# A graph-attention layer and a graph convolution in one kernel: values by seven block products after the keys, and two running sums in the softmax

## The chip, the cores and the metric

The kernel runs on one core of a Trainium2 chip. A core has a matrix engine (TensorE, PE in the profile; PEld are its weight loads), a vector engine (VectorE, DVE), a scalar engine (ScalarE, ACT), GpSimd (POOL) and SyncE (SP), which here issues most DMAs. The metric is device time in microseconds, taken as the median of several runs. All arithmetic is fp32.

## The reference, cut to what matters

Input x has 16 batches of 1024 nodes with 256 channels; adj is 1024 x 1024. Two layers follow each other. The part that the change touches is in layer 0:

```python
h = relu(layernorm(x))
fea = h.transpose(0, 2, 1)                     # batch, channel, node
c_adj = mean(fea, axis=1)
diff = c_adj[:, None, :] - c_adj[:, :, None]
A = abs(abs(sigmoid(diff) - 0.5) - 0.5) * 2    # A_s = (A + A^T) / 2
g = relu(einsum('bcn,bnm->bcm', fea, adj * A_s) * para)
q = g by heads                                  # 4 heads of 64 channels
k, v = halves of h @ kv_w by heads              # kv_w is 256 x 512
out = softmax(q @ k^T * scale) @ v
x = x + out
```

Layer 1 normalises x again, multiplies it with the normalised adjacency matrix, then with W1 (512 x 256), applies a batch norm over all batches and nodes, a relu, W2 and another batch norm, and adds the result to x.

## The kernel before, in words

A first stage runs over the 16 batches and does layer 0 of each batch together with the adjacency product and W1 of the batch before; a second stage does the rest of layer 1, for which all batches must be done. The order of the instructions on every engine is written out by hand (a manual schedule): an engine executes its instructions in the order in which the code issues them, and buffers and semaphore waits are placed by the framework. A buffer of a pool is taken when its tile is first written, and is free again when the last reader of the tile before is done.

One turn of the batch loop has these steps.

- **Attention** (`attention`). There are four steps: two halves of the 512 queries times two pairs of heads. In each, `scores` makes eight blocks of 128 keys by 2 heads by 512 queries in PSUM (L743, two heads at once on half of PE's rows each), ACT takes the exponential into a tile p (L751), and DVE adds the eight tiles into one running sum (L757 for the first two, L760 for the six after). `partial` turns that sum in blocks of 32 (L768) and reduces it (L776). `values` in `attention` multiplies p with v (L784), and DVE turns the result (L797). The weights of the next batch's graph product are begun between (`hooks`: ACT at L353 and L356, DVE at L361).
- **The graph product of the next batch** (`graph_seven`, from the third batch on; `graph` for the first two). The product of h and the weights is made from six blocks in pairs, by seven products instead of eight (Strassen's method in Winograd's form: sums of the blocks are made on DVE, and one PSUM bank, f_gpsx, collects several products and is copied by ACT in between, at L641, L653 and L659). Its results are joined by DVE (L661, L664, L667) and multiplied with para into the queries (L670, L683).
- **Values and keys of the next batch**, at the end of `graph_seven`. Values come first: the function `values` at L443 takes 128-node blocks of h (turned, in hT) as the stationary operand and the 256 value columns of kv_w as the moving one, 16 matmuls of 256 columns in two PSUM tiles, which ACT copies (L458). Keys follow in seven products of 128 x 128 by 128 x 512 blocks (L691): sums of the key weights (`sums`, loaded by L537 from `kvs_d`, where `make_key_sums` puts them once, L1019) times sums of h (kt1 to kt4, made by DVE at L677 to L681). The bank f_kpsx collects four of these products and is copied by ACT after each (L707, L713, L718, L725); the next product into it waits for the copy. On ACT, the relu of the second layer norm (`norm.relu`, L281) stands before these copies; it needs `norm.shifts` (L266) of DVE.
- **Adjacency product and W1 of this batch** (`linear1`, L944, and `linear1_seven`, L1050), again by seven products. The layer norm of the batch after the next is prepared in it.

SP issues, in this order within `graph_seven`: loads of the sums, hT, para, the key sums and three adjacency sums; sixteen small DMAs that turn the attention result (f_att, L852); then, after the keys' second product, the store of the batch's x (`leave`, L1195) and a load of a later x (`arrive`, L191).

PSUM has one pool of three two-bank tiles (`ps_s`, used by scores, f_gps, f_vps, f_kpsx, the adjacency product) and two single banks (`ps_t` and `ps_o`). In SBUF the change touches the pools' tags "acc" (two buffers), "att" and "sums" (one each).

Of the kernel before, what the change touches and what calls it, by code (L numbers as in the profile page):

```python
# [10 lines left out]
F32 = mybir.dt.float32  # L11
# [6 lines left out]
P = 128  # L18
# [11 lines left out]
def fast_path(  # L30
# [20 lines left out]
    nc = tc.nc  # L51
# [3 lines left out]
    NC = N // P  # L55
# [7 lines left out]
    dram = ctx.enter_context(tc.tile_pool(name="fdram", bufs=1, space=DRAM))  # L63
# [3 lines left out]
    hT_d = [dram.tile([CC, P, N], F32, tag=f"fhT_{b}", name=f"fhT_{b}") for b in range(B)]  # L67
    gs_d = [dram.tile([P, 12, P], F32, tag=f"fgs_{b}", name=f"fgs_{b}") for b in range(B)]
    w1s_d = dram.tile([P, 4, FC * P // 2], F32, tag="fw1s", name="fw1s")
    kvs_d = dram.tile([P, 4, P], F32, tag="fkvs", name="fkvs")  # L70
    t_d = [dram.tile([P, 4, 512], F32, tag=f"ft_{k}", name=f"ft_{k}") for k in range(3)]
    z1_d = [dram.tile([P, FC, 512], F32, tag=f"fz1_{t}", name=f"fz1_{t}") for t in range(TT)]

# [102 lines left out]
    with ExitStack() as stage:  # L176
# [266 lines left out]
        def values(b, hT, v):  # L443

            copies = []
            for c4 in range(0, NC, 4):
                ps = ps_s.tile([P, 4, C], F32, tag="s", name=f"f_vps_{b}_{c4}")
                for i in range(4):
                    for e in range(CC):
                        nc.tensor.matmul(  # L450
                            ps[:, i, :],
                            hT[e][:, ts(c4 + i, P)],
                            kvw_t[:, e, C : 2 * C],
                            start=(e == 0),
                            stop=(e == CC - 1),
                        )
                copies.append(
                    lambda c4=c4, ps=ps: nc.scalar.copy(v[:, c4 : c4 + 4, :], ps)  # L458
                )
            return copies  # L460
# [40 lines left out]
        def graph_seven(b, left, norm, load_more, last):  # L501
# [32 lines left out]
                hT.append(t)  # L534
            qT = big.tile([P, CC, N], F32, tag="qT", name=f"f_qT_{b}")
            nc.sync.dma_start(qT, para_v)
            nc.sync.dma_start(sums, kvs_d)  # L537
            load_more()
            kT = big.tile([P, CC, N], F32, tag="kT", name=f"f_kT_{b}")
            v = big.tile([P, NC, C], F32, tag="v", name=f"f_v_{b}")  # L540
# [114 lines left out]
            m4(2)  # L655
            for n in range(PAIRS):
                m5(n)
            t23 = pp.tile([P, 2, 512], F32, tag="acc", name=f"f_kt23_{b}", bufs=2)
            nc.scalar.copy(room[:, 1], x)  # L659
            add0()  # L660
            nc.vector.tensor_add(room[:, 2], room[:, 2], m7)  # L661
            norm.stats(0, 4)
            norm.invert(0, 4)
            nc.vector.tensor_add(room[:, 3], room[:, 1], m7)  # L664
            both = lambda d: room[:, 2 * d : 2 * d + 2].rearrange("p n k -> p (n k)")
            for d in range(CC):
                nc.vector.tensor_add(both(d), both(d), gps[d])  # L667
# [1 line left out]
                ws.pop((b, c))  # L669
            nc.vector.tensor_mul(qT[:, 0, :], both(0), qT[:, 0, :])  # L670
            norm.shifts(0, 4)
            norm.relu(0, 4, False)
            copy0, copy1 = values(b, hT, v)
            copy0()
            kt2, kt3, kt4 = t23[:, 0], t23[:, 1], rest[:, 0]
            part = lambda k, j: hT[k][:, ts(j, 512)]
            nc.vector.tensor_sub(kt3, part(1, 1), part(0, 1))  # L677
            nc.vector.tensor_add(kt2, kt3, part(0, 0))
            nc.vector.tensor_sub(kt4, part(1, 0), kt2)
            kt1 = part(0, 1)  # L680
            nc.vector.tensor_sub(kt1, kt1, part(0, 0))  # L681
            add1()
            nc.vector.tensor_mul(qT[:, 1, :], both(1), qT[:, 1, :])  # L683
            norm.stats(4, NC)
            norm.invert(4, NC)


            aw = lambda i, k: kvw_t[:, k, ts(i, P)]

            def mult(ps, left, right, more=False):  # L690
                nc.tensor.matmul(  # L691
                    ps, left, right, start=not more, stop=True, skip_group_check=more
                )

            c = lambda i, j: kT[:, i, ts(j, 512)]
            x = ps_s.tile([P, 512], F32, tag="s", name=f"f_kpsx_{b}")
            m7 = ps_s.tile([P, 512], F32, tag="s", name=f"f_kps7_{b}")
            k2 = ps_t.tile([P, 512], F32, tag="t", name=f"f_kps2_{b}")
            k4 = ps_o.tile([P, 512], F32, tag="o", name=f"f_kps4_{b}")

            def relu_queries(d):

                nc.scalar.activation(qT[:, d, :], qT[:, d, :], AF.Relu, scale=-SCALE)

            todo = [lambda d=d: relu_queries(d) for d in range(CC)]
            mult(x, aw(0, 0), part(0, 0))
            nc.scalar.copy(c(0, 0), x)  # L707
            mult(k2, aw(0, 1), part(1, 0))
            nc.vector.tensor_add(c(0, 0), c(0, 0), k2)
            leave(b - 1)  # L710
            arrive(b + 1)
            mult(x, sums[:, 1], kt2, True)
            nc.scalar.copy(c(1, 0), x)  # L713
            todo.pop(0)()
            mult(m7, sums[:, 2], kt3)
            nc.vector.tensor_add(c(1, 0), c(1, 0), m7)
            mult(x, sums[:, 0], kt1, True)
            nc.scalar.copy(c(1, 1), x)  # L718
            copy1()
            mult(k4, aw(1, 1), kt4)  # L720
            nc.vector.tensor_add(c(1, 1), c(1, 1), m7)
            norm.shifts(4, NC)
            nc.vector.tensor_add(c(1, 0), c(1, 0), k4)
            mult(x, sums[:, 3], part(1, 1), True)
            nc.scalar.copy(c(0, 1), x)  # L725
            if last:
                todo.pop(0)()
            else:
                norm.relu(4, NC, False)
            return (qT, kT, v), todo  # L730

        def attention(b, qT, kT, v, hooks):

            steps = [(g, pair) for g in range(NH) for pair in range(HEADS // 2)]
            p_of, acc_of, oT_of, o_of, red_of = {}, {}, {}, {}, {}

            def scores(s, within=None):
                g, pair = steps[s]
                for m in range(NC):
                    ps = ps_s.tile([P, 2, 512], F32, tag="s", name=f"f_s_{b}_{s}_{m}")  # L740
                    for e in range(2):
                        rows_e = slice(e * HD, (e + 1) * HD)
                        nc.tensor.matmul(  # L743
                            ps[:, e, :],
                            kT[rows_e, pair, ts(m, P)],
                            qT[rows_e, pair, ts(g, 512)],
                            start=True,
                            stop=True,
                        )
                    p = pp.tile([P, 2, 512], F32, tag="p", name=f"f_p_{b}_{s}_{m}")  # L750
                    nc.scalar.activation(p, ps, AF.Exp)  # L751
                    p_of[s, m] = p
                    if m == 1:
                        acc = pp.tile(
                            [P, 2, 512], F32, tag="acc", name=f"f_acc_{b}_{s}", bufs=2
                        )
                        nc.vector.tensor_add(acc, p_of[s, 0], p)  # L757
                        acc_of[s] = acc
                    elif m > 1:
                        nc.vector.tensor_add(acc_of[s], acc_of[s], p)  # L760
                    if m == 5 and within:
                        within()

            def partial(s):

                g, pair = steps[s]
                t = ow.tile([P, 2, 16, 32], F32, tag="sums", name=f"f_sums_{b}_{s}")
                nc.vector.transpose(  # L768
                    t.rearrange("p e j i -> p (e j i)"),
                    acc_of.pop(s).rearrange("p e q -> p (e q)"),  # L770
                )
                if pair == 0:
                    red_of[g] = small.tile(
                        [P, HEADS // 2, 2, 16], F32, tag="red", name=f"f_red_{b}_{g}", bufs=1
                    )
                nc.vector.tensor_reduce(red_of[g][:, pair], t, AX.X, ALU.add)  # L776
# [89 lines left out]
            first = finish(0)  # L866
            collect, invert, spread, scale, add = first
            for i in range(len(steps)):
                scores(i, collect if i == 2 else None)
                for step in hooks.get(i, ()):  # L870
                    step()
                if i == 2:
                    invert()
                    spread()
                partial(i)
                if i == 2:
                    scale()
                values(i)
# [139 lines left out]

        def make_key_sums():  # L1019

            t = pp.tile([P, 2, 512], F32, tag="acc", name="f_kvs", bufs=2)
            s1, s2, s3, s4 = (t[:, 0, ts(n, P)] for n in range(4))
            a = lambda i, k: kvw_t[:, k, ts(i, P)]
            nc.vector.tensor_add(s1, a(1, 0), a(1, 1))
            nc.vector.tensor_sub(s2, s1, a(0, 0))
            nc.vector.tensor_sub(s3, a(0, 0), a(1, 0))
            nc.vector.tensor_sub(s4, a(0, 1), s2)
            nc.sync.dma_start(kvs_d.rearrange("p n q -> p (n q)"), t[:, 0])

        def load_w1_sums(b):  # L1030
            t = pp.tile([P, 4, FH * P], F32, tag="p", name=f"f_w1s_{b}")
# [459 lines left out]
    with ExitStack() as stage:  # L1491
# [21 lines left out]
        with tc.manual_schedule(engines={ENG.PE, ENG.Activation, ENG.DVE, ENG.Pool, ENG.SP}):  # L1513
# [7 lines left out]
            def bank(name, pool=None):  # L1521
                return (pool or ps_z).tile([P, 512], F32, tag="z", name=name)
# [31 lines left out]
            class Pair:  # L1554
# [46 lines left out]
                def add(self, j, c, ps):  # L1601
                    nc.vector.tensor_add(place(self.t[j], c), place(self.t[j], c), ps)
# [768 lines left out]
```

## Time and profile before

| what | value |
|---|---|
| median of 3 runs | 2397.92 us (2396.44 to 2398.54) |
| profiled execution, its span | 2396.9 us |
| PE busy | 2353.8 us, 98% |
| DVE busy | 1974.2 us, 82% |
| ACT busy | 1346.8 us, 56% |
| one turn of the batch loop (723 to 855 us and its neighbours) | about 131 us |
| granted clock of TensorE, mean | 0.995 |

The profiled execution's own time is its span; the median of the runs is 1.0 us longer. In the profile a matmul's record is longer than the spacing of matmuls that follow each other, since they overlap: PE's busy share says that there are few gaps, not that each is at its peak. An fp32 product appears as two matmul records with a weight load each. Where a list of instructions shows idle time in brackets, it is the idle time of the engine before that group, and what ended it. The chain of work that ended last is followed back from the last instruction.

### The profile page before, as it was taken

What the parts mean: (1) busy time and instruction counts of PE and PEld (TensorE: products, weight loads), DVE (VectorE), ACT (ScalarE), POOL (GpSimd) and SP (SyncE); (2) the same over time, 40 slices, a digit from 0 to 9 for tenths busy, and PEclk for the clock granted to TensorE, in tenths of its full rate; (3) what the DMA queues carried; (4) which work ended last, traced back from release to release, by engine and by line L of the source; (5) the groups of instructions that cost most, each with busy time, mean ns of one, the idle gap of its engine ahead of it and who ended that gap; (6) DMA issues with size and microseconds to landing.
All of it is one profiled execution on the core that took longest, in us unless ns stands there. A gap on an engine that the chain in (4) does not pass through costs nothing.

```text
span 2396.9 us, 24478 instructions
## 1 busy us (share of the span) xinstructions
PE 2353.8 (98%) x7950; PEld 1032.4 (43%) x7950; DVE 1974.2 (82%) x2806; ACT 1346.8 (56%) x1974; POOL 174.1 (7%) x253
## 2 busy tenths in 40 slices
PE   8999999999999999999999999999999999999995
PEld 4443444434343434444343434344443434444444
DVE  6888889797979798897979797988979798757766
ACT  6845555564736455555647374555555565346654
POOL 2030010101010000101010100001010100000000
PEclk9999999999999999999999999999999999999998
DMA  5042433433342434334323414243433321355569
GB/s 189 8 143 93 144 116 123 136 117 91 98 156 64 160 93 160 100 123 136 120 96 111 140 61 164 87 167 93 137 123 121 115 85 53 114 208 181 174 243 371
DMA packets 178650, 312.44 MB, mean 130 GB/s; under 512 B 33617, under 2 KB 117073, under 8 KB 178513
## 3 DMA queue, kind: packets, MB, share of 16 engines
q1 hardware_dynamic: 164176, 267.25, 33.2%
q0 software_dynamic: 9728, 26.76, 3.7%
q10 hardware_dynamic: 4608, 16.78, 1.7%
q8 instruction: 65, 1.06, 0.2%
q14 instruction: 73, 0.59, 0.1%
HBM read 195.04 MB, written 96.79 MB: 122 GB/s over the span
## 4 chain that ended last, share of the span: by engine, by line
PE 72%; DVE 18%; ACT 4%; issue 3%; DMA 1%; SPq 1%; DVEq 0%; ACTq 0%; POOLq 0%; POOL 0%
PE f_aps L944 16%; PE f_s L743 12%; PE f_o L784 11%; PE f_zps L1050 6%; DVE f_acc L760 6%; PE f_vps L450 5%; PE f_zx L1588 4%; DVE f_w L361 4%; PE f_gpsx L576 3%; PE f_zm L1588 3%; ACT f_p L751 3%; PE f_gps L576 3%; PE f_kpsx L691 2%; PE f_gps L404 2%; PE f_kps L691 2%
## 5 line engine op out<-in xcount | busy, mean ns | idle before, releaser
L751 ACT ACTIVATE f_p<-f_s 128x1024 f32<-128x1024 f32 x512 | 477.4, 1048 | 163.0 <-PE f_s L743 163.0
L760 DVE TENSOR_TENSOR f_acc<-f_acc,f_p 128x1024 f32<-128x1024 f32 x384 | 470.5, 1225 | 41.4 <-DVE f_acc L760 1.4
L743 PE MATMUL f_s<-f_qT,f_kT 64*128 64x512 f32 x2048 | 457.1, 596 | 0.0
L784 PE MATMUL f_o<-f_p,f_v 128*64 128x512 f32 x2048 | 453.6, 595 | 0.0
L743 PEld LDWEIGHTS f_s<-f_qT,f_kT 64*128 64x128 f32 x2048 | 190.2, 185 | 264.4 <-ACT f_p L751 118.6
L784 PEld LDWEIGHTS f_o<-f_p,f_v 128*64 128x64 f32 x2048 | 141.4, 137 | 304.4 <-issue 251.3
L353 ACT ACTIVATE f_w<-f_row,f_col 128x1024 f32<-128x1024 f32 x127 | 147.0, 1157 | 31.6 <-PE f_gps L514 16.8
L361 DVE SCALAR_TENSOR_TENSOR f_w<-f_w,f_adj 128x1024 f32<-128x1024 f32 x127 | 152.7, 1212 | 4.2 <-ACT f_w L356 4.2
L260 POOL TENSOR_TENSOR f_rstd_b<-f_var_b,f_mhalf 128x4 f32<-128x4 f32 (+1 forms) x31 | 33.1, 1069 | 1502.3 <-DVE f_var_b L259 1502.3
L356 ACT ACTIVATE f_w<-f_w 128x1024 f32<-128x1024 f32 x127 | 134.3, 1058 | 4.0
L944 PE MATMUL f_aps<-f_ahatT,f_hs 128*128 128x512 f32 x256 | 115.1, 592 | 0.0
L944 PE MATMUL f_aps<-f_ahatT,f_h_b 128*128 128x512 f32 x256 | 113.4, 596 | 0.0
L450 PE MATMUL f_vps<-f_kvw,f_hT 128*128 128x256 f32 x512 | 113.1, 379 | 0.0
L944 PE MATMUL f_aps<-f_t,f_hs 128*128 128x512 f32 x256 | 112.5, 592 | 0.0
L281 ACT ACTIVATE f_h_b<-f_x,f_shift_b,f_rstd_b 128x256 f32<-128x256 f32 x128 | 66.3, 593 | 75.7 <-DVE f_shift_b L266 75.7
L450 PEld LDWEIGHTS f_vps<-f_kvw,f_hT 128*128 128x128 f32 x512 | 97.3, 190 | 20.1 <-issue 7.4
L281 ACT ACTIVATE f_h_a<-f_x,f_shift_a,f_rstd_a 128x256 f32<-128x256 f32 x126 | 73.8, 587 | 50.5 <-DVE f_shift_a L266 50.5
L514 PE MATMUL f_gps<-f_w,f_h_a 128*128 128x512 f32 x224 | 99.9, 599 | 0.0
L757 DVE TENSOR_TENSOR f_acc<-f_p,f_p 128x1024 f32<-128x1024 f32 x64 | 76.3, 1192 | 14.4 <-ACT f_p L751 14.4
L576 PE MATMUL f_gps<-f_w,f_h_a 128*128 128x512 f32 x168 | 82.7, 601 | 3.8 <-DVE f_w L361 3.8
L1073 ACT ACTIVATE f_z<-f_zps,f_b 128x512 f32<-128x512 f32 x60 | 38.0, 683 | 75.3 <-PE f_zps L1050 75.3
L776 DVE TENSOR_REDUCE f_red<-f_sums 128x32 f32<-128x1024 f32 x64 | 78.1, 1220 | 2.2
(275 smaller groups left out, 3410.6 us busy)
## 6 DMA issues: line engine op xcount, KB each, us to landing
f_t<-ft SPq DMA_DIRECT2D x84, 512.0 KB, 10.9
fz<-f_z SPq DMA_DIRECT2D x64, 512.0 KB, 9.6
f_x<-in_x_dram SPq DMA_DIRECT2D x31, 1024.0 KB, 6.3
f_zb<-fz SPq DMA_DIRECT2D x42, 512.0 KB, 4.2
f_att<-f_oT SPq DMA_DIRECT2D x512, 32.0 KB, 1.9
fx<-f_x SPq DMA_DIRECT2D x16, 1024.0 KB, 4.4
fhT<-f_hQ POOLq DMA_DIRECT2D x112, 128.0 KB, 2.9
f_hT<-fhT SPq DMA_DIRECT2D x28, 512.0 KB, 6.0
```

What stands on the lines that cost most here:

```text
L281: nc.scalar.activation(self.h[:, c, :], self.xt[:, c, :], AF.Relu, bias=self.shift[:, c : c + 1], scale=self.rstd[:, c : c + 1], accum_out ...
L353: nc.scalar.activation(w, rows[b], AF.Abs, bias=cols[b][:, c : c + 1], scale=0.5 / C)
L361: nc.vector.scalar_tensor_tensor(w, w, 1.0, adj_t[c], ALU.subtract, ALU.mult)
L450: nc.tensor.matmul(ps[:, i, :], hT[e][:, ts(c4 + i, P)], kvw_t[:, e, C : 2 * C], start=(e == 0), stop=(e == CC - 1),)
L576: nc.tensor.matmul(ps, left, right, start=fresh and n == 0, stop=(n == PAIRS - 1), skip_group_check=more,)
L743: nc.tensor.matmul(ps[:, e, :], kT[rows_e, pair, ts(m, P)], qT[rows_e, pair, ts(g, 512)], start=True, stop=True,)
L751: nc.scalar.activation(p, ps, AF.Exp)
L760: nc.vector.tensor_add(acc_of[s], acc_of[s], p)
L784: nc.tensor.matmul(o_of[s][e * HD : (e + 1) * HD, :], v[:, m, ts(2 * pair + e, HD)], p[:, e, :], start=(m == 0), stop=(m == NC - 1),)
L944: nc.tensor.matmul(ps, left[:, m, :], right(m), start=not more and m == 0, stop=(m == KH - 1), skip_group_check=more,)
L1050: nc.tensor.matmul(ps[i], left[:, ts(i, P)], right, start=not more, stop=True, skip_group_check=more,)
L1588: nc.tensor.matmul(ps, left[:, m, :], right[:, m, :], start=start and m == 0, stop=(m == 1), skip_group_check=not start,)
```

## The change

From the third batch on (`graph_seven`) three things differ.

1. **Values by seven products.** They are made as the keys are, with sums of the value weights (`sums_v`, a new load from `kvs_d`, which now holds eight sums per partition instead of four) and the same sums of h. The sums of h are now the stationary operand, in four blocks of 128 nodes, and the 128 weight columns are the moving one: each product is four matmuls of 128 columns into one bank. ACT copies four times, DVE adds four times.
2. **Order and buffers.** Keys come first, directly after the graph product, and values behind them. The sums of h (kt1 to kt4) are made earlier on DVE, between the steps that join the graph product. The relu of the second layer norm is cut in two, `norm.relu(0, 2)` behind the keys' second copy and `norm.relu(2, 4)` behind the third. t23 moves to the tag "att", and sums_v takes its place in "acc". The keys' collecting bank and the bank of product 7 lie in one tile of `ps_s`, and the values use two more tiles.
3. **Two running sums in `attention`.** The p tiles 0, 1, 4, 6 are added into acc, the tiles 2, 3, 5, 7 into a second tile, and at the end the second is added to the first. The second tile uses the buffer of the tag "sums", into which `partial` then writes. The steps that stood between `scores` and `partial` (`hooks`, `invert`, `spread`) are issued before that last addition.

The diff, cut to its core:

```diff
@@ graph_seven
-            t23 = pp.tile([P, 2, 512], F32, tag="acc", name=f"f_kt23_{b}", bufs=2)
+            sums_v = pp.tile([P, 4, P], F32, tag="acc", name=f"f_kvs_{b}", bufs=2)
+            nc.sync.dma_start(sums_v, kvs_d[:, 4:8])
             nc.scalar.copy(room[:, 1], x)
             add0()
+            t23 = ow.tile([P, 2, 512], F32, tag="att", name=f"f_kt23_{b}")
+            kt2, kt3, kt4 = t23[:, 0], t23[:, 1], rest[:, 0]
+            part = lambda k, j: hT[k][:, ts(j, 512)]
+            nc.vector.tensor_sub(kt3, part(1, 1), part(0, 1))
+            nc.vector.tensor_add(kt2, kt3, part(0, 0))
             nc.vector.tensor_add(room[:, 2], room[:, 2], m7)
             norm.stats(0, 4)
             norm.invert(0, 4)
+            kt1 = part(0, 1)
+            nc.vector.tensor_sub(kt1, kt1, part(0, 0))
             nc.vector.tensor_add(room[:, 3], room[:, 1], m7)
+            nc.vector.tensor_sub(kt4, part(1, 0), kt2)
...
             norm.shifts(0, 4)
-            norm.relu(0, 4, False)
-            copy0, copy1 = values(b, hT, v)
-            copy0()
...
+            product(K, 1)
+            K.copy(0, 0)
+            product(K, 2)
+            product(K, 6)
+            K.copy(1, 0)
+            norm.relu(0, 2, False)
+            product(K, 7)
+            product(K, 5)
+            K.copy(1, 1)
+            norm.relu(2, 4, False)
+            product(K, 4)
+            K.add(0, 0, 2)
+            K.add(1, 0, 7)
             add1()
+            leave(b - 1)
+            arrive(b + 1)
             nc.vector.tensor_mul(qT[:, 1, :], both(1), qT[:, 1, :])
...
+            product(K, 3)
+            K.copy(0, 1)
+            todo.pop(0)()
+            K.add(1, 1, 7)
+            K.add(1, 0, 4)
             norm.stats(4, NC)
             norm.invert(4, NC)
+            product(V, 1)
+            V.copy(0, 0)
+            product(V, 7)
+            product(V, 6)
+            V.copy(1, 0)
+            product(V, 4)
+            product(V, 5)
+            V.copy(1, 1)
+            product(V, 2)
+            V.add(1, 0, 7)
             norm.shifts(4, NC)
+            V.add(1, 0, 4)
+            V.add(1, 1, 7)
+            V.add(0, 0, 2)
             if last:
                 todo.pop(0)()
             else:
                 norm.relu(4, NC, False)
+            product(V, 3)
+            V.copy(0, 1)
@@ class Seven, new: one product of the values
+                    for n in range(4):
+                        nc.tensor.matmul(
+                            ps[:, n],
+                            right[:, ts(n, P)],
+                            left,
+                            start=not more and n == 0,
+                            stop=n == 3,
+                            skip_group_check=True,
+                        )
@@ product, new: m is K or V
+                left, right = {
+                    1: (m.w(0, 0), part(0, 0)),
+                    2: (m.w(0, 1), part(1, 0)),
+                    3: (m.s[:, 3], part(1, 1)),
+                    4: (m.w(1, 1), kt4),
+                    5: (m.s[:, 0], kt1),
+                    6: (m.s[:, 1], kt2),
+                    7: (m.s[:, 2], kt3),
+                }[n]
+                into = "x" if n in (1, 3, 5, 6) else n
+                m.mult(m.ps[into], left, right, n in (3, 5, 6))
@@ attention, scores
-                    elif m > 1:
-                        nc.vector.tensor_add(acc_of[s], acc_of[s], p)
+                    elif m == 3:
+                        odd = ow.tile([P, 2, 16, 32], F32, tag="sums", name=f"f_sums_{b}_{s}")
+                        odd_of[s] = odd
+                        flat = odd.rearrange("p e j i -> p e (j i)")
+                        nc.vector.tensor_add(flat, p_of[s, 2], p)
+                    elif m > 3:
+                        to = flat if m % 2 else acc_of[s]
+                        nc.vector.tensor_add(to, to, p)
...
+                for step in before_last:
+                    step()
+                nc.vector.tensor_add(acc_of[s], acc_of[s], flat)
@@ make_key_sums
+            t = pp.tile([P, 8, P], F32, tag="acc", name="f_kvs", bufs=2)
+            for n in range(2):
+                s1, s2, s3, s4 = (t[:, 4 * n + q] for q in range(4))
+                a = lambda i, k: kvw_t[:, k, ts(2 * n + i, P)]
...
+            nc.sync.dma_start(kvs_d, t)
```

`K.copy` and `V.copy` are copies of the collecting bank by ACT, `K.add` and `V.add` additions of another bank by DVE, and `todo.pop(0)()` is the relu of one half of the queries on ACT.

## The prediction

> **What bounds the kernel now.** I read the page's busy shares first, then the chain of work that ended last over one batch's seam (806 to 822 us), then the timelines of ScalarE (ACT) and VectorE (DVE) there, then the seam's start (795 to 798 us), where TensorE (PE) stalls.
>
> The page, busy time; then the chain over the seam (start, duration, piece):
>
> ```profile
> PE 2353.8 (98%) x7950; PEld 1032.4 (43%) x7950; DVE 1974.2 (82%) x2806; ACT 1346.8 (56%) x1974; POOL 174.1 (7%) x253
> ...
> 806.89 6.91 PE f_vps L450 x32
> 813.80 0.86 PE f_kpsx L691 x2
> 814.66 0.86 PE f_kps L691 x2
> 815.52 0.98 PE f_kpsx L691 x2
> ```
>
> PE carries the whole chain. Values take 32 matmuls in 6.91 us, 0.216 each at 256 columns; one key product is two passes of 512 columns, 0.858. A product that adds into the bank just copied takes 0.98 or 0.94, because its weights can't be loaded ahead. So PE's own time, plus any wait of PE, is the kernel's time; other engines count only where PE waits for them.
>
> ACT in the seam, with what ended its idle time in brackets:
>
> ```profile
> 806.93 0.58 ACT L659 COPY f_v<-f_gpsx 128x512 f32<-128x512 f32 x1 [3.71 <-PE f_gpsx L576]
> 811.87 2.08 ACT L281 ACTIVATE f_h_b<-f_x,f_shift_b,f_rstd_b 128x256 f32<-128x256 f32 x4 [4.35 <-DVE f_shift_b L266]
> 813.85 0.99 ACT L458 COPY f_v<-f_vps 128x1024 f32<-128x1024 f32 x1
> 814.74 0.58 ACT L707 COPY f_kT<-f_kpsx 128x512 f32<-128x512 f32 x1
> 817.02 1.06 ACT L703 ACTIVATE f_qT<-f_qT 128x1024 f32<-128x1024 f32 x1
> ```
>
> and DVE:
>
> ```profile
> 807.55 0.69 DVE L664 TENSOR_TENSOR f_v<-f_v,f_gps 128x512 f32<-128x512 f32 x1 [1.80 <-ACT f_v L659]
> 808.27 2.35 DVE L667 TENSOR_TENSOR f_v<-f_v,f_gps 128x1024 f32<-128x1024 f32 x2
> 810.54 1.22 DVE L670 TENSOR_TENSOR f_qT<-f_v,f_qT 128x1024 f32<-128x1024 f32 x1
> 811.68 0.16 DVE L266 SCALAR_TENSOR_TENSOR f_shift_b<-f_mv_b,f_rstd_b 128x4 f32<-128x4 f32 x1
> ```
>
> The relu L281 waits 4.35 us for the shifts L266, and the shifts sit behind L664, which waits for PE's last graph product. Today this wait is free: PE does the values meanwhile.
>
> The seam's start, PE then DVE, and two weight loads in a row:
>
> ```profile
> 797.19 1.12 PE L576 MATMUL f_gps<-f_w,f_h_a 128*128 128x512 f32 x2 [0.56 <-DVE f_w L361]
> ...
> 795.91 1.22 DVE L361 SCALAR_TENSOR_TENSOR f_w<-f_w,f_adj 128x1024 f32<-128x1024 f32 x1
> ...
> 818.97 0.30 PEld L691 LDWEIGHTS f_kpsx<-f_hT,f_kt 128*128 128x128 f32 x2 [0.65 <-ACT f_kT L718]
> ```
>
> Here PE does wait for DVE, once per batch. In the waits table this is 3.8 us in 14; a record (0.592) outlasts the spacing (0.429), so add 14 x 0.163, and 14 x 0.104 for loads not done ahead: 7.6 us in all. The two loads span 0.30, the second 0.19 of it: a load occupies 0.108.
>
> **What the Trainium skill says.** "TensorE: Matmul & The Clock Gate", step-by-step: weight loads are pulled ahead of running matmuls. The trace agrees: at 256 columns 0.216 is the stream alone. The same page, LDWEIGHTS section: columns / 1.2 ns, 107 for 128; measured 0.108. "PSUM", engine vs sequencer instructions: ScalarE is strict FIFO. So a copy behind a waiting relu waits too.
>
> **Part 1, values in seven products.** Removed: 32 matmuls of 256 columns, 6.91 us per batch. Added: 7 products x 4 blocks x 2 passes = 56 of 128 columns. No fp32 row with 128 moving columns and a full-price load exists here. Below: the stream is 0.107 (half of 0.214), and the transposes of 128 columns are spaced 0.110 (eight in 1.04, the last record 0.273), though with cheaper loads. Above: the same skill page, back-to-back gap, gives 81 ns for paired 128-column bf16 matmuls against 56 alone, so 25 more: an estimate of 0.135. A pessimist's bound is 0.19, the whole load record. I take 0.110, since load 0.108 and stream 0.107 overlap: 56 x 0.110 = 6.16, so -0.75 us per batch.
>
> **Part 2, the new order.** Times below count from 806.73, the first values matmul. PE now starts keys at 0; m1 is "K1" and so on. From the trace: a copy starts 0.245 after its product's stream ends, takes 0.58 (the next ACT op 0.49 after its start), and PE's load follows 0.05 after its end.
> K1 ends 0.86. K2's bank is f_gpsx's, copied until 0.79: load 0.84, end 1.80. K6 waits for copy 1.10-1.68: end 2.70. K7 3.56. K5, copy 2.95-3.53: end 4.55. K4 5.41.
> K3 needs the third copy, which could begin at 4.79. But norm.relu(0, 2) stands ahead of it on ACT, and needs the shifts. DVE: L664 at 0.82, the new kt4 +0.61, the two gps adds +0.61 and +1.14, L670 +1.14, shifts +1.13: 5.43, done 5.59 (today 5.10). Relus 5.63 and 6.13 (spacing 0.50), copy 6.63-7.20, K3 loads 7.26, ends **8.22**; without the hold 6.39. The hold costs 1.83 us.
> Values: V1 ends 9.10; its copy stands behind the copy of K3 (8.47) and relu_queries (8.96, next op 9.93): 9.93-10.51. V7 ends 9.98, V6 loads 10.56, ends 11.55: 0.58 late. V4 12.43, V5 (copy wait) 13.42, V2 14.30, V3 15.28. Today the same stretch takes 13.26. So **+2.02 us per batch**: values -0.75, key waits 2.22 against 0.35, value waits 0.90. Times 14: **+28.3**.
>
> Hidden, each with its cover: kt3, kt2 and kt1 fill DVE's idle stretches before L661 (1.61) and L664 (1.80); uncovered they cost 2.1 per batch. The four value adds on DVE (2.4) run under linear1, where DVE is busy 24 of 36 us. sums_v's DMA stands on SP behind sixteen f_att issues, the last at 0.83; queues are idle then, 256 KB takes 3.8, so it lands near 5.2 against need at 9; behind it are x1's store (today issued at 9.0) and the x load, neither delayed. Four more DVE adds in make_key_sums (0.3-0.6 each, once) and its doubled DMA precede a step with slack. V's banks come from gps, free at 4.4. The next x's relu (4 to 8) ends about 16.2, 0.9 into linear1 (today 2.7).
>
> **Part 3, two running sums.** Still seven adds per step. Chained ones are spaced 1.33 (six L760 in 7.87), independent ones about 1.14 (L667: two in 2.35). DVE saves up to 0.9 per step, limited by exp's pace of 0.90. PE never waits for DVE inside attention, so nothing there. But at the last step DVE runs without a gap into the graph stage: f_o's transpose starts at 782.64 as the op before ends, while PE's f_o ended at 780.98. By its last step's exps (third odd input ready 771.83) DVE arrives 1.18 earlier, 0.8 in batches that begin later. The 0.56 stall and its slow loads should go: up to -7.6, I take **-7.3** (between 0 and -7.6).
>
> Sum: 28.3 - 7.3 = +21.0 on a span of 2396.9, 2417.9; the runs' median is 1.0 above that span, so **2419 us**.
>
> **Rivals.**
> (a) Loads aren't hidden well, 0.135: values +1.4 per batch, part absorbed by V6's wait, so +0.85: +12, 2431. For: load and stream are equal in length. Against: two loads follow each other at 0.108 and the second stream follows without gap. With 0.19 about 2470.
> (b) Faster: no hold. Had the shifts, reckoned to end at 5.59, ended by 3.75, both relus (1.0) would be through before the third copy could begin at 4.79; then +2.02 - 1.83 = +0.19 per batch, +2.7 - 7.3 = -4.6: 2393. With a hold of 0.33 the change comes out even (14 x 0.52 = 7.3), so the point of decision is an end of the shifts at 4.1. Against: four DVE ops of 4.6 us follow L664, and L664 waits for PE.
> (c) DVE's gain doesn't reach PE (ACT or a buffer holds masked L361): 2426. For: ACT's differences precede it. Against: they end 3.4 us before L361 starts.
> (d) The sums could stay chained by a wait on the buffer "sums"; that only gives (c).
>
> **Chances.** Forecast 0.52 (its own range 2411 to 2427), slower loads 0.18, (c) 0.08, (b) with a little beyond 0.22. The range for all: 2394 to 2434; below lies about 0.12 of (b), above about 0.07 of the slow loads. No change is within 0.2%, 4.8 us, about what a measurement can tell: (b) spreads around its edge, 0.15 faster and 0.07 same; the rest, 0.78, slower.
>
> **What would show it.** Right: ACT's first relu L281 of the pair about 2 us idle before it, the third kpsx copy after it, PE's last key product with a wait near 1.8 us; f_vps matmuls spaced 0.110; L576's wait for L361 gone; L760 spaced 1.14. Wrong: matmul spacing at 0.13 or above; key products all near 0.98; the shifts L266 ending under 4.1 us after the last graph product. The forecast fails on the good side if ACT's copies pass before the relu, on the bad one if the loads show.

## The result, and the profile after

The changed kernel takes **2471.89 us** (median of 5 runs, 2470.37 to 2473.15) against 2398.37 us (2396.44 to 2399.53) for the kernel before: a ratio of 1.0309, 95% interval 1.0297 to 1.0321. It is slower, as forecast, but by 73.5 us where 21 were forecast, and it lies above the range. The profiled execution spans 2471.3 us.

The page of the changed kernel, busy time of the engines:

```profile
PE 2354.2 (95%) x8286; PEld 1038.1 (42%) x8286; DVE 1990.2 (81%) x2866; ACT 1352.5 (55%) x2002; POOL 179.0 (7%) x253
```

TensorE (PE) is busy 2354.2 us, 0.4 more than before, in a span that is 74.4 us longer. So the time is waits of PE. The waits table of the changed kernel names them (engine, its line, what it waited for: us in total, times, longest):

```profile
PE f_vps L706 <- DVE f_v L719: 27.7, 14, 2.0
PE f_kps L701 <- DVE f_kT L719: 22.5, 14, 1.6
PE f_vps L706 <- ACT f_v L716: 17.0, 14, 1.2
PE f_adjps L1301 <- DMA f_adj<-in_adj_dram: 9.8, 1, 9.8
PE f_kps L701 <- ACT f_kT L716: 9.5, 14, 0.7
```

Four of these waits come once in each of the 14 batches, 76.7 us together. The load of `adj` at the start of the span stood in the kernel before too (9.7). Gone is this wait of the graph product for VectorE (DVE), from the waits table of the kernel before:

```profile
PE f_gps L576 <- DVE f_w L361: 3.8, 14, 0.6
```

The chain of waits over one batch's seam, from the graph product to the aggregation (start, duration, piece; lines between left out); the first key matmul starts at 828.75:

```profile
833.04 1.22 DVE f_qT L679
834.26 0.09 DVE f_shift_b L266
...
834.37 1.09 ACT f_h_b L281 x2
835.46 0.48 ACT f_kT L716
835.94 0.02 issue
835.96 0.70 DVE f_kT L719
836.66 0.04 issue
836.70 1.14 PE f_kps L701 x2
...
839.30 0.59 ACT f_v L716
839.89 0.04 issue
839.93 3.90 PE f_vps L706 x32
...
843.86 0.59 ACT f_v L716
844.45 0.02 issue
844.47 0.69 DVE f_v L719
845.16 0.09 DVE f_shift_b L266
845.25 0.02 issue
845.26 1.29 DVE f_v L719 x2
846.56 0.14 issue
846.70 1.13 PE f_vps L706 x8
```

Before, PE carried this stretch alone. Now the chain leaves it for the hold that the prediction describes (shifts L266, relu L281, copy L716), but the piece that releases PE at 836.70 is not that copy: it is a DVE addition, L719, of product 7, a product whose bank PE does not touch next. The same at 846.70: product 3 of the values collects in x, and an addition from product 7's bank releases it. The timeline of ACT, DVE and PE shows what those additions themselves had waited for (in brackets, idle time before and what ended it):

```profile
832.25 1.13 PE L701 MATMUL f_kps<-f_kt,f_kt 128*128 128x512 f32 x2 [0.68 <-ACT f_kT L716]
834.18 0.15 DVE L266 SCALAR_TENSOR_TENSOR f_shift_b<-f_mv_b,f_rstd_b 128x4 f32<-128x4 f32 x1
835.36 0.56 ACT L716 COPY f_kT<-f_kps 128x512 f32<-128x512 f32 x1
835.96 0.69 DVE L719 TENSOR_TENSOR f_kT<-f_kT,f_kps 128x512 f32<-128x512 f32 x1 [1.03 <-ACT f_kT L716]
839.93 2.05 PE L706 MATMUL f_vps<-f_kvs,f_kt 128*128 128x128 f32 x16 [1.22 <-ACT f_v L716]
```

The first line is product 7 of the keys. Nothing had to be read from its own bank, yet it waits for ACT's copy of x, the other bank of the same tile. The addition from bank 7 at 835.96 waits for the copy of x begun at 835.36. The addition only reads from this tile, and so does the copy. So in the tiles shown here each use waits for the use before it, whichever bank that was, a read behind a read too.

### The profile page after: what moved, and what is told of

The parts are those of the page before. It is cut to its first block, busy times and chain, and to the rows that moved or that the text cites. A ratio compares the mean times of both kernels' runs of the same rounds, so it can differ in the third digit from the quotient of the medians.

```text
span 2471.3 us, 25199 instructions
## 1 busy us (share of the span) xinstructions
PE 2354.2 (95%) x8286; PEld 1038.1 (42%) x8286; DVE 1990.2 (81%) x2866; ACT 1352.5 (55%) x2002; POOL 179.0 (7%) x253
## 4 chain that ended last, share of the span: by engine, by line
PE 87%; DVE 4%; DMA 3%; ACT 3%; issue 2%; SPq 0%; ACTq 0%; DVEq 0%; POOLq 0%; POOL 0%
PE f_s L810 18%; PE f_o L860 18%; PE f_aps L1019 16%; PE f_zps L1126 6%; PE f_gps L576 5%; PE f_zx L1664 4%; PE f_gpsx L576 4%; PE f_gps L514 4%; PE f_zm L1664 3%; PE f_vps L706 3%; PE f_gps L404 2%; DVE f_v L719 1%; DMA f_t<-ft 1%; PE f_z2ps L1602 1%; DMA f_z<-fx 1%
## 5 line engine op out<-in xcount | busy, mean ns | idle before, releaser
L833 DVE TENSOR_TENSOR f_acc<-f_acc,f_p 128x1024 f32<-128x1024 f32 x128 | 155.9, 1218 | 4.5 <-ACT f_p L818 4.5
L833 DVE TENSOR_TENSOR f_sums<-f_sums,f_p 128x1024 f32<-128x1024 f32 x128 | 155.8, 1217 | 0.0
L1019 PE MATMUL f_aps<-f_ahatT,f_hs 128*128 128x512 f32 x256 | 115.1, 592 | 0.0
L1019 PE MATMUL f_aps<-f_ahatT,f_h_b 128*128 128x512 f32 x256 | 113.6, 597 | 0.0
L1019 PE MATMUL f_aps<-f_t,f_hs 128*128 128x512 f32 x256 | 112.5, 592 | 0.0
L281 ACT ACTIVATE f_h_a<-f_x,f_shift_a,f_rstd_a 128x256 f32<-128x256 f32 x126 | 73.8, 587 | 50.5 <-DVE f_shift_a L266 50.5
L281 ACT ACTIVATE f_h_b<-f_x,f_shift_b,f_rstd_b 128x256 f32<-128x256 f32 x128 | 67.8, 593 | 55.9 <-DVE f_shift_b L266 55.9
L830 DVE TENSOR_TENSOR f_sums<-f_p,f_p 128x1024 f32<-128x1024 f32 x64 | 78.3, 1223 | 23.2 <-ACT f_p L818 23.2
L844 DVE STREAM_TRANSPOSE f_sums<-f_acc 128x1024 f32<-128x1024 f32 x64 | 79.7, 1245 | 2.2
L576 PE MATMUL f_gps<-f_w,f_h_a 128*128 128x512 f32 x168 | 81.2, 592 | 0.0
```

Source lines behind the costliest of these rows:

```text
L281: nc.scalar.activation(self.h[:, c, :], self.xt[:, c, :], AF.Relu, bias=self.shift[:, c : c + 1], scale=self.rstd[:, c : c + 1], accum_out ...
L576: nc.tensor.matmul(ps, left, right, start=fresh and n == 0, stop=(n == PAIRS - 1), skip_group_check=more,)
L833: nc.vector.tensor_add(to, to, p)
L1019: nc.tensor.matmul(ps, left[:, m, :], right(m), start=not more and m == 0, stop=(m == KH - 1), skip_group_check=more,)
```

## The experiments

Theory **T**: the banks of one two-bank tile are ordered as one, so PE waits for copies and additions of the other bank. Rival **H**: the waits come from the order on ACT and DVE alone (the hold of the prediction, larger than reckoned), and the tiles play no part. The prediction's rivals (a), slow weight loads, and (c), no gain from the sums, are tested on the way. For each kernel I also give the **stretch**: the mean over 14 batches from the first matmul of keys and values to the first one of the work after them (the aggregation; in the last batch the scores), from PE's matmul records. It is the sum of keys and values; in the row of the forecast, keys and values are the prediction's.

| kernel | time, us | keys | values | stretch |
|---|---|---|---|---|
| before | 2398.37 | 6.31 | 6.91 | 13.21 |
| changed | 2471.89 | 8.91 | 10.06 | 18.97 |
| forecast for it | 2419 | 8.22 | 7.06 | 15.28 |
| before_pair | 2450.19 | 10.05 | 6.91 | 16.96 |
| apart_v | 2427.41 | 8.91 | 6.94 | 15.85 |
| apart_kv | 2416.62 | 8.19 | 6.94 | 15.13 |
| relu_behind | 2469.73 | 7.84 | 10.27 | 18.11 |
| plain_behind | 2428.58 | 8.91 | 6.91 | 15.83 |
| sums_only | 2390.79 | 6.31 | 6.91 | 13.21 |
| apart_relu | 2401.40 | 6.98 | 7.05 | 14.02 |
| swap_banks | 2393.11 | 6.26 | 7.16 | 13.42 |
| swap_adds | 2390.62 | 6.26 | 7.02 | 13.28 |
| swap_end | 2384.29 | 6.26 | 6.57 | 12.83 |

### The values' banks in tiles of their own

```diff
-            for n in range(2):
-                pair = ps_s.tile([P, 2, 512], F32, tag="s", name=f"f_vps_{b}_{n}")
-                for m, at in ((("x", 0), (7, 1)), ((4, 0), (2, 1)))[n]:
-                    V.ps[m] = V.bank(pair, at)
+            for m, pool, tag in (("x", ps_s, "s"), (7, ps_t, "t"), (4, ps_o, "o"), (2, ps_s, "s")):
+                V.ps[m] = V.bank(pool.tile([P, 512], F32, tag=tag, name=f"f_vps{m}_{b}"))
```

> Values' four collecting banks (x, 7, 4, 2) each in a tile of its own instead of two pairs in two two-bank tiles; orders and instructions unchanged. Theory T (the two banks of one tile are ordered as one: a product into one bank waits for the copy or the addition that reads the other bank): the values' stretch falls from 10.0 us to about 7.1 us, 14 batches by 2.9 us are 41 us, so about 2431 us. Rival H (the late copies come from the order on ScalarE and VectorE alone, the tile plays no part): nothing changes, 2472 us.

2427.41 us (2426.87 to 2428.30; 1.0123 of before, 1.0106 to 1.0139): 44.5 us less than the changed kernel, without one instruction moved. Values fall from 10.06 to 6.94 us, where the forecast's steps had 7.06. So H falls for the values.

### And the keys' banks

```diff
-            pair = ps_s.tile([P, 2, 512], F32, tag="s", name=f"f_kps_{b}")
-            K.ps["x"], K.ps[7] = pair[:, 0], pair[:, 1]
+            K.ps["x"] = ps_s.tile([P, 512], F32, tag="s", name=f"f_kpsx_{b}")
+            K.ps[7] = ps_s.tile([P, 512], F32, tag="s", name=f"f_kps7_{b}")
```

> As apart_v, and the keys' banks x and 7 too in tiles of their own. Theory T: the keys' stretch falls by a further 0.7 us a batch, that is 10 us, so about 2421 us, which is the forecast of 2419 us within what the rows allow. Rival H: 2472 us.

2416.62 us (2416.06 to 2417.27; 1.0076, 1.0059 to 1.0093), 2.4 us under the forecast and 55.3 us under the changed kernel. The pairs' cost in the stretch is 14 times (18.97 - 15.13) = 53.8 us. The chain of waits in this kernel's seam (first key matmul at 811.86):

```profile
817.28 0.17 DVE f_shift_b L266
817.45 0.02 issue
817.48 1.09 ACT f_h_b L281 x2
818.57 0.48 ACT f_kT L716
819.04 0.04 issue
819.09 1.14 PE f_kpsx L701 x2
```

This is the forecast's hold as it was written: shifts, two relus, the third copy, product 3. Product 3 starts at 819.09 - 811.86 = 7.23 us (forecast 7.26), and now the copy itself releases it: H falls for the keys too. One wait is new, in the waits table:

```profile
PE f_kps L701 <- DVE f_v L676: 7.9, 14, 0.6
```

Product 7's own tile takes a buffer that the gate's sums still hold until L676 has read them. The hold swallows this wait, because product 3 can't start before 7.2 in any case; the pair had spared it, at the price measured here.

### The kernel before with the keys' banks paired

```diff
-            x = ps_s.tile([P, 512], F32, tag="s", name=f"f_kpsx_{b}")
-            m7 = ps_s.tile([P, 512], F32, tag="s", name=f"f_kps7_{b}")
+            pair = ps_s.tile([P, 2, 512], F32, tag="s", name=f"f_kpsx_{b}")
+            x, m7 = pair[:, 0], pair[:, 1]
```

> The kernel before, with the keys' banks x and 7 put into one two-bank tile and nothing else changed. Theory T: the seventh product and the third wait for copies and additions of the other bank, and the keys' stretch grows by 2 to 3.5 us in each of 14 batches, so 2426 to 2446 us. Rival H (banks of one tile are independent): 2398 us.

2450.19 us (2446.85 to 2452.04; 1.0216, 1.0199 to 1.0233): +51.7 us from the tile alone, above T's upper end by 4. Its waits table, for the keys:

```profile
PE f_kpsx L691 <- DVE f_kT L716: 21.9, 14, 1.6
...
PE f_kpsx L691 <- ACT f_kT L713: 9.5, 14, 0.7
```

PE's timeline over one batch, products 7, 5 and 3 of the keys, first in the kernel before, then in before_pair (product 4, which no wait precedes, left out):

```profile
816.34 1.02 PE L691 MATMUL f_kps<-f_kt,f_kt 128*128 128x512 f32 x2
817.19 1.11 PE L691 MATMUL f_kpsx<-f_hT,f_kt 128*128 128x512 f32 x2
...
819.00 1.10 PE L691 MATMUL f_kpsx<-f_hT,f_kt 128*128 128x512 f32 x2
```

```profile
695.32 1.13 PE L691 MATMUL f_kpsx<-f_kt,f_kt 128*128 128x512 f32 x2 [0.68 <-ACT f_kT L713]
698.01 1.13 PE L691 MATMUL f_kpsx<-f_hT,f_kt 128*128 128x512 f32 x2 [1.56 <-DVE f_kT L716]
...
700.53 1.13 PE L691 MATMUL f_kpsx<-f_hT,f_kt 128*128 128x512 f32 x2 [0.54 <-DVE f_kT L721]
```

Product 7 waits for ACT's copy of x, as in the changed kernel. The long wait is that of product 5, not of product 3 as T's forecast had it: in the order of this kernel the addition from bank 7 (L716) is issued ahead of product 5. Product 3 waits for the next addition from bank 7 (L721; in the waits table 4.9 us in 9 batches). That the two sums in the table, 9.5 and 21.9, are nearly those of the keys in the changed kernel (9.5 and 22.5) is chance for the second. There the addition is late by the hold; here no relu holds it, and it stands behind DVE's own queue (in this kernel's chain a residual addition, a gate product and the norm's statistics). So the pair makes such waits without the hold and with values first. In a batch at full clock product 7 starts 0.83 us later than in the kernel before, product 5 another 1.84 and product 3 another 0.70; that is 3.41 us a batch, 47.7 in 14. The other 4.8 us of the stretch's 52.5 (14 times 3.75) are a lower clock in some batches, told at the end.

The traces also say who does the ordering, since they keep the semaphore that a weight load waits for, and which engine counts it up. Engine waited for by the first weight load of a key product, the same in all 14 batches:

| kernel | product 7 | product 5 | product 3 |
|---|---|---|---|
| before | PE itself | ACT | ACT |
| before_pair | ACT | DVE | DVE |
| changed | ACT | DVE | DVE |
| apart_kv | PE itself | ACT | ACT |

With the banks apart, the load of product 7 waits for PE itself; paired, it waits for ACT. These waits are in the program, and a bank that shares its tile has other ones. The Trainium skill ("PSUM — Partial Sum Buffer", section on bank collisions) says that two engines must be kept apart on one bank and quadrant of partitions, two readers included, while different banks run clean. So by the page no wait between the two banks was needed. The trace of apart_kv agrees: PE's records of the values' product 4 (823.32 to 824.38) and ACT's copy of x (823.52 to 824.10) overlap, and the two kernels with banks apart are 44.5 and another 10.8 us faster.

### The relus behind the values' copies, tiles as in the changed kernel

```diff
             K.copy(1, 0)
-            norm.relu(0, 2, False)
...
             K.copy(1, 1)
-            norm.relu(2, 4, False)
...
             V.copy(0, 0)
+            norm.relu(0, 2, False)
...
             V.copy(1, 0)
+            norm.relu(2, 4, False)
```

> The changed kernel with the two groups of relus of the queries' norm moved behind the values' first and second copies, tiles unchanged: this takes away what holds the keys' third copy. The forecast's hold alone: 1.83 us a batch back, 26 us, so 2446 us. Theory T: the third product still waits for the addition from the other bank of its tile, which comes behind the shifts on VectorE, so only about 1.0 us a batch comes back, 14 us, about 2457 us.

2469.73 us (2469.24 to 2471.41): 2.2 us less, and neither number. The keys do what T says, 8.91 to 7.84 us, 15.0 us in 14 batches: product 3 still waits for the addition behind the shifts, only less. Values take 0.21 more on average, so 12.0 remain, though in batches at full clock they take the same 10.00 us in both kernels. Some 10 of the 12 are given back behind the stretch, where no engine is waited for. Two windows of this kernel, one batch's last value products and the aggregation after them (window: length, PE busy and matmuls, granted clock, DMA share, GB/s):

```profile
564.00:572.00 8.00, 5.68 (x47) 0.98 0.28 94
572.00:577.00 5.00, 5.00 (x11) 0.68 0.75 250
```

In the second the granted clock is 0.68. In 8 of 14 batches the first matmuls of L1019 last 1.06 instead of 0.59 us and stand 0.85 apart instead of 0.43; PE's spacing there exceeds the usual by 9.8 us in all, against 1.1 in the changed kernel. So the move was worth 15 us in waits, near T's 14, and the clock took most of it back.

### Values as before, behind the keys

Here the values are the plain 16 products again, in the changed order; h's second block has to be restored for them by one more addition on DVE.

```diff
+            nc.vector.tensor_add(kt1, kt1, part(0, 0))
...
-            product(V, 1)
-            V.copy(0, 0)
-            product(V, 7)
...
+            copy0, copy1 = values(b, hT, v)
+            copy0()
...
+            copy1()
```

> The changed kernel with values' projection put back to the plain 16 products of 256 columns, left behind the keys (an added addition brings h's block back from kt1). This is the order and the softmax's sums alone, without block products and without the values' two pairs. Keys' stretch as in the changed kernel, 8.9 us, values 6.9 us: 15.8 us a batch against 13.3 us before, 14 times 2.5 us less 6.3 us for the sums, so about 2428 us. If the block products themselves cost the time (weight loads of 128 columns not hidden, rival (a)), the same number; the two are told apart by the spacing of values' products in the changed kernel. If the order costs nothing: 2392 us.

2428.58 us (2427.38 to 2429.19; 1.0130, 1.0114 to 1.0145), as expected. With sums_only below this splits the 73.5 us: the sums -6.9, the order and the keys' pair +37.8 (in the stretch 14 times 2.62, 36.7), the seven products of the values with their pairs +43.3 (in the stretch 14 times 3.14, 44.0). The three add up to 74.2, since the kernel before took 2397.72 us in the comparison of sums_only. With apart_v beside it: in their own banks the block products take as long as the plain ones, 6.94 against 6.91.

### The running sums alone

```diff
-                    elif m > 1:
-                        nc.vector.tensor_add(acc_of[s], acc_of[s], p)
+                    elif m == 3:
...
+                        nc.vector.tensor_add(flat, p_of[s, 2], p)
+                    elif m > 3:
+                        to = flat if m % 2 else acc_of[s]
+                        nc.vector.tensor_add(to, to, p)
```

> The kernel before with part 3 alone: two alternating running sums, the next group's steps of the norm issued ahead of the last addition; values' projection untouched. The forecast: the 7.1 us of waits ahead of the gate's products of 168 instructions goes, 2391 to 2392 us. Rival (c) of the prediction (VectorE's gain does not reach TensorE): 2398 us.

2390.79 us (2389.85 to 2391.21) against 2397.72 in the same comparison: 0.9970, 0.9959 to 0.9981. The gain is 6.9 us where 7.3 were forecast, and rival (c) is out.

### Towards a version that beats both

Four steps on top of apart_kv, each aimed at a wait left in the trace of the one before. First, both groups of relus of the norm behind the values' first two copies, and the queries' relu behind the first:

```diff
             K.copy(1, 0)
-            norm.relu(0, 2, False)
...
             K.copy(1, 1)
-            norm.relu(2, 4, False)
...
             K.copy(0, 1)
-            todo.pop(0)()
...
             V.copy(0, 0)
+            todo.pop(0)()
+            norm.relu(0, 2, False)
...
             V.copy(1, 0)
+            norm.relu(2, 4, False)
```

> As apart_kv (all six collecting banks in tiles of their own), with the two groups of relus of the queries' norm moved behind the values' first two copies and the relus of the queries behind the values' first copy: all that apart_kv left of the keys' and values' waits on ScalarE. Theory T with the forecast's hold (1.83 us) and the late first copy (0.6 us): 14 times 2.4 us less than apart_kv's 2416.6 us, 2383 to 2387 us, below the kernel before. If these waits are hidden or come back elsewhere: 2405 to 2417 us.

2401.40 us (2400.77 to 2402.58; 1.0016, 1.0009 to 1.0023): 15.2 of the 30 to 34 us. The hold is gone, and two waits that it had covered set the end now, as the waits table of apart_relu shows:

```profile
PE f_kps L701 <- DVE f_v L676: 7.9, 14, 0.6
...
PE f_vps L706 <- DVE f_kT L719: 5.4, 14, 0.4
```

The first cost nothing while the hold was there, the second is the bank of product 4, which the keys' addition frees late. So the banks of products 4 and 7 were exchanged:

```diff
-            K.ps[7] = ps_s.tile([P, 512], F32, tag="s", name=f"f_kps7_{b}")
...
-            K.ps[4] = ps_o.tile([P, 512], F32, tag="o", name=f"f_kps4_{b}")
+            K.ps[7] = ps_o.tile([P, 512], F32, tag="o", name=f"f_kps7_{b}")
+            K.ps[4] = ps_s.tile([P, 512], F32, tag="s", name=f"f_kps4_{b}")
```

> As apart_relu, with two of the keys' banks exchanged: product 7 collects in the bank that the gate's seventh product left (free early), product 4 in the bank that the gate's sums held until the addition into room. In the trace of apart_relu product 7's first weight load waits 0.73 us for that addition, and product 4 of the values waits 0.55 us for an addition from product 4 of the keys. If each of these waits sets the end: the first goes, 14 times 0.73 us are 10 us, so about 2391 us. If the time comes back at a later wait: 2396 to 2401 us.

2393.11 us (2392.60 to 2394.22; 0.9979, 0.9970 to 0.9988): 8.3 of 10 us. Then the keys' last two additions were moved ahead on DVE:

```diff
             add1()
+            K.add(1, 1, 7)
+            K.add(1, 0, 4)
             leave(b - 1)
             arrive(b + 1)
...
-            K.add(1, 1, 7)
-            K.add(1, 0, 4)
```

> As swap_banks, with the keys' last two additions on VectorE moved ahead of the previous batch's residual addition and the gate's product, so that the bank of the values' fourth product is free earlier. If both waits of apart_relu set the end: 14 times 0.73 and 0.55 us, 18 us less than 2401.4 us, so about 2384 us, below the kernel before (2398 us) and below sums_only (2391 us). If the second wait was already gone with the exchange of the banks: as swap_banks.

2390.62 us (2390.16 to 2392.11; 0.9969, 0.9958 to 0.9980): only 2.5 of some 8 us, level with sums_only. Product 4's bank is free, but the next wait was right behind it:

```profile
PE f_vpsx L706 <- ACT f_v L716: 5.0, 14, 0.4
```

Product 5 waits for the values' second copy, which stands behind the queries' relu (1.06 us) on ACT. That relu is needed only for the scores, after the aggregation (in the last batch, where the other half's relu moves with it, the scores follow at once):

```diff
             V.copy(0, 0)
-            todo.pop(0)()
...
             V.copy(0, 1)
+            todo.pop(0)()
```

> As swap_adds, with the relus of the queries (1.06 us on ScalarE) moved from behind the values' first copy to behind their last, so that the second copy, which the fifth product waits for, is not held. The trace of swap_adds shows 0.52 and 0.10 us ahead of that product in a batch: 14 times 0.6 us are 8.7 us, so about 2382 us, below sums_only (2391 us). If ScalarE's next work (the relus of the norm, the aggregation's) then comes late instead: 2388 to 2391 us.

**2384.29 us** (2384.09 to 2386.11; 0.9947, 0.9934 to 0.9961), below the kernel before and below sums_only. In the chain over one seam PE stands alone:

```profile
806.42 0.86 PE f_kps L701 x2
807.28 0.94 PE f_kpsx L701 x2
808.22 0.89 PE f_vpsx L706 x8
...
812.83 0.89 PE f_vps L706 x8
```

In 13 of the 14 batches no wait is left, and the seven products take 6.44 us, 0.47 less than the plain ones. In the last batch PE waits 1.6 us for the moved relu, so the mean is 6.57. The kernel is 6.5 us below sums_only; by the gain of each over the kernel before in its own comparison, 12.7 and 6.9, it is 5.8.

## Why the prediction was wrong, step by step

- **Part 1, the spacing of 0.110: right.** The values' matmuls in the changed kernel are spaced 0.112 (starts at 837.774, 837.886, 837.997; 0.1116 on average), so 56 take 6.25 us and not 6.16. Rival (a) is out. Its 2470 for a spacing of 0.19 comes within 2 us of the result, by accident: the total can't tell these causes apart, the spacing can.
- **Part 2, the hold: right.** The shifts start 834.18 - 828.75 = 5.43 us into the stretch (forecast 5.43), the third copy at 835.36, so 6.61 (6.63). Rival (b) needed the shifts at 4.1.
- **Part 2, the walk along the products: the step that failed.** "K7 3.56", "K3 loads 7.26", "V7 9.98" and "V3 15.28" let a product start as soon as PE had reached it and its own bank was read. The change description in this document names the shared tiles, and the steps used them as separate banks. In the trace product 7 of the keys loads at 832.25, 3.50 after the start instead of 2.70, behind the copy of x; product 3 at 836.70, so 7.95 instead of 7.26, behind an addition from bank 7; the values' product 7 at 839.93, so 11.18 instead of 9.10; their product 3 at 846.70, so 17.95 instead of 14.30. Summed, the stretch is +5.76 us and not +2.02. With the tiles apart it is +1.92: 15.13 against the 15.28 of those steps, and 2416.62 us against 2419. There product 7 of the keys is late too (3.39 instead of 2.70, the gate's buffer), which the walk had at nothing and the hold covers: that this miss cost nothing is luck. The term that was missing, the waits through a shared tile, is 55.3 us.
- **The fault compounds.** An addition waits for a copy of the other bank, and a product waits for that addition. In the changed kernel the keys' addition also stands behind the shifts on DVE and the values' additions have the second layer norm's shifts between them (845.16 in the chain). So here a wait that goes through two engines picks up both queues.
- **The hidden work: right.** The earlier sums of h and the load of sums_v appear in no wait of PE in the changed kernel.
- **Part 3: right.** -7.3 forecast, -6.9 measured alone. The wait of L576 is gone, and additions in `attention` start 1.14 apart where they stood 1.33 apart (median 1.136 against 1.329).
- **The range.** Its upper end was built from slow weight loads alone. A wait through a shared tile was considered only for the softmax's buffer, in (d), not for the collecting banks, where the steps of PE, ACT and DVE meet in one tile.

## What to carry to other kernels

When work is reckoned product by product, list for each not only its operands but every earlier use of the *tile* that it writes, on every engine: two banks in one tile bought a saved buffer here, and cost 55 us in waits between accesses that had nothing to do with each other. These waits are part of the program, so it pays to look at what each weight load is made to wait for before its start is reckoned. And a wait that costs nothing may only be covered by a longer one: of the 2.4 us a batch that the ACT order seemed to hold in apart_kv, 1.1 came back at first, and the rest only after three more waits had been moved.

## What the runs showed that was not expected

Waits of PE of 1 to 2 us, repeated within a stretch, can cost more than their length, where a lower granted clock comes with them. In before_pair the matmuls of the last key products stand 0.85 apart in 5 of 14 batches (the median stretch is 16.62, the mean 16.96), in relu_behind the first ones of the aggregation in 8. The changed kernel has as many waits, and this in one batch only; the kernel before, apart_kv and swap_end have no such matmul in the batch loop. The Trainium skill ("TensorE: Matmul & The Clock Gate", section "What's actually happening") ties half the clock to an idle window of some 3.4 us; the longest single wait in a stretch here is 2.0 us, in the waits table of the changed kernel.

The clock records of the traces show more. In the batch loops of all twelve kernels the clock falls to half 15 times, each time for 3.413 us, and each of these pieces starts a whole number of times 3.413 us after the trace's first clock record. So the time can be cut into such pieces ahead of any wait. Two neighbouring pieces each from two batches of relu_behind (window: length, PE busy and matmuls, granted clock, DMA share, GB/s):

```profile
568.35:571.76 3.41, 1.43 (x13) 1.00 0.00 0
571.76:575.17 3.41, 3.41 (x9) 0.50 0.54 172
1524.08:1527.49 3.41, 1.51 (x14) 1.00 0.00 0
1527.49:1530.91 3.42, 3.33 (x14) 1.00 0.37 94
```

The first piece of each pair is partly empty, never wholly; only after the emptier one does the clock fall. Counting PE's records without the 0.163 us by which each outlasts the spacing (0.592 - 0.429), PE fills at most 43% of the piece ahead in all 15 cases, and at least 44% of every other of the 7468 pieces. So by these traces it is not the length of one wait that counts but how much of one piece the waits leave empty, and a partly busy piece is enough, where the page speaks of an idle one. The same count tells the kernels apart: the changed kernel's turn of 136.47 us is nearly 40 pieces (136.53), so its waits fall on the pieces almost alike in batch after batch, and after the first batch none is emptied that far. A turn of relu_behind without a fall takes 135.41 us, so its waits shift against the pieces, and 9 of 14 batches meet a fall (the ninth in the last batch's scores). This was read from the traces afterwards; no run was made to test it.
